# Variance of a head from a sum of squares and a column of the gates product, and column sums of two weights in other tiles

## The chip, the cores and the metric

The kernel runs on one core of one Trainium2 chip. The metric is the device time of one execution in microseconds (us). The engines are TensorE (PE; PEld is its loading of weights), VectorE (DVE), ScalarE (ACT), GpSimd (POOL) and SyncE (SP), which issues the DMA transfers.

## What is computed

One decoder layer in fp32 on x of 16 x 256 x 512, in three parts, each followed by a layer norm without parameters:

```python
x = _layernorm(x + attn(x))            # a state space block: projections, convolution, scan, output product
x = _layernorm(x + xattn(x, k, bias, ctx))   # long convolutions of v*x2 by k, contracted with x1
x = _layernorm(x + ffn(x))             # base product, plus low-rank updates of the best 2 of 8 experts
```

The layer norm and the last part, which the change touches, are

```python
m = mean(x); v = var(x); (x - m) / sqrt(v + 1e-5)
base   = x_flat @ W.T + b
logits = x_flat @ gate_w.T + gate_b
gates  = softmax(top_k(logits, 2))
out    = base + sum over the two experts of gate * (x_flat @ lora_A.T) @ lora_B.T
```

## The kernel before

**Two stages.** The first (the first 766 us or so) is the state space block over 8 groups of 512 tokens, with its layer norm; its result goes to DRAM. The second is a loop over 32 heads (`h`); a head is 8 channels of the sequence for all 16 batches, so it has 128 rows of 512. It does the long convolution of the head as matmuls, the contraction, the second layer norm, and the feed-forward part with the third norm. The order of instructions on each engine is that of the source (the schedule is manual). Buffers rotate within pools: a tile that takes a buffer waits for the readers of the one before.

**A round of the head loop** works on three heads. For head h it convolves two halves of the batches, q = 0 and q = 1, into four PSUM banks `y0`, `y1` (two each). Each half begins with a seed product (`seeded`, L1006, into `y1`), whose result ACT copies into another block (`spread_seed`, L1010). Then PE does four full products (L1021) and twelve quadrant products (L1036); the last quadrants wait for a tiny ACT copy `one` (L1052). DVE contracts a half with two products with the context (`multiplied`, L1071, `y1` first) and two reductions (`reduced`, L1081). As there is one set of `y` banks, the seed of one half waits until the products of the half before have read `y1`. For head h+1 DVE forms `kv` (`products`, L155), and POOL forms `xs` (twice, L991), the difference of filters `Td` (L996) and the skip products `sk` (L927).

For head h-1 the round finishes the second half: POOL adds `ol` (L1229), which holds its output with channels on partitions: four chunks of 128 channels by 128 rows. The mean over channels needs no subtraction from `ol`: the weights `w_f` (of the base product) and `w_gl` (8 gate columns and 128 low-rank columns) have had their column means removed once, in group 1 of the first stage. What is left of the second layer norm is one scale per row, `rs`, from the variance. For this, `centre` (L1175) transposes the four chunks of `ol` on PE (`transposed`, L1108, identity as the weights' partner), so that a row lies along a partition; ACT sums the transposed rows (L1181), POOL makes the negative mean `nm_b` (L1094), ACT squares the centred rows and sums (L1099), and POOL forms `var_b` (L1101) and its power of -1/2, `rs_b` (L1102). The POOL work of the next residual (`skip_term` L944, `with_residual` L958 and L962) stands between `nm_b` and `var_b`, or behind `rs_b`.

Then PE does the gates product `gl` (L1272: four chunks, 136 columns) and the base product (L1196, in parts around the seed). `gates` on DVE scales the logits (`lg`, L1115), takes their maximum (L1117), ranks them by three comparisons of 64 elements (`cmp`, L1124 to L1126) and a reduction (L1128), zeroes the exponentials of all but two (`ex`, L1130), and scales the low-rank product (`xa`, L1135). In the next round `xa` is transposed (L1186), copied by ACT (L1188) and multiplied into `base` (L1192); `finish` forms `x3` with its sum on DVE (L1148), then the centred square of the third norm, by the same `centred_squares` (L1094 to L1102 with tag c), and `store` writes the result (L1158, L1159). The last head has its own code after the loop, with transposes and a statistics instruction of DVE.

**The column means** are formed by `chunk_sum` (POOL, L525 and L527) and `centred` (PE L533 into the PSUM tile `mw`, DVE L535), called in group 1 at i = 3 to 6. The sums lie in two of the six rotating buffers of tag `acc`; the convolutions of the first stage (ACT L578, DVE L580 and L582) use the same six. `mw` is one of two buffers of the pool `ps_t`, which `head_means` (PE L593, `xm`) and others use.

Of the kernel before, what the change touches and what calls it, by code (L numbers as in the profile page):

```python
# [10 lines left out]
ALU = mybir.AluOpType  # L11
# [39 lines left out]
    (3, 1, 1), (2, 1, 1), (1, 1, 1), (0, 1, 1),  # L51
)
ER = NE * R
WARM = 8


# [14 lines left out]
def decoder_kernel(  # L71
# [108 lines left out]
    with ExitStack() as s1:  # L180
# [7 lines left out]

        xg = x.rearrange("b (c p) d -> (b c) p d", p=P)
        xTg = xT.rearrange("(k p) n -> p k n", p=P)  # L190
        NG = NTOK // GT

        def load_x(g):
            xs = []
# [326 lines left out]

        def chunk_sum(w, cols):

            total = p2.tile([P, D], F32, tag="acc", name="w_sum", bufs=6)[:, 0:cols]
            nc.gpsimd.tensor_tensor(total, w[:, 0, :], w[:, 1, :], ALU.add)  # L525
            for kc in range(2, KD):
                nc.gpsimd.tensor_tensor(total, total, w[:, kc, :], ALU.add)  # L527
            return total

        def centred(w, cols, total):  # L530

            ps = ps_t.tile([P, 512], F32, tag="tr", name="mw")
            nc.tensor.matmul(ps[:, 0:cols], share, total, start=True, stop=True)  # L533
            for kc in range(KD):
                nc.vector.tensor_tensor(w[:, kc, :], w[:, kc, :], ps[:, 0:cols], ALU.subtract)  # L535

        def normalised(g, *ts):

# [5 lines left out]

        heads = {}
        late, sums = [], []
        for g in range(NG):
            xs = xs_next
            more = g + 1 < NG
            if not more:  # L550
                load_w_o(0, 1)
                cTs = [load_c(0), load_c(1)]
# [92 lines left out]
            for i, (kind, p) in enumerate(order):  # L645
                if g == 1 and i == 2:
                    with_identity(w_f)
                if g == 1 and i in (3, 4):
                    w, cols = ((w_f, D), (w_gl, NE + ER))[i - 3]
                    total = chunk_sum(w, cols)  # L650
                if g == 1 and i in (5, 6):
                    centred(*sums.pop(0))
                if g == 1 and i in (3, 4):
                    sums.append((w, cols, total))
                if i == 6:
                    ms = [head_means(0)]
                if g == 0 and i == 0:
                    al, be = first_products(
                        kinds[kind], p, True, None,
                        lambda: begun.append(begin_products(w_xi, order[1][1], False)),  # L660
                    )
                else:
                    al, be = first_products(
                        kinds[kind], p, i % 3 == 0, begun.pop(0) if begun else None
                    )
                if i == 8:
                    ms.append(head_means(1))
                if i == 9:


                    yps = ps_t.tile([P, S], F32, tag="tr", name="yps")
                    for ht in range(HT):
                        for b in range(GB):
                            nc.tensor.matmul(
                                yps[b * HP : (b + 1) * HP],
                                sel[:, ht].rearrange("p q h -> p (q h)"),
                                Bs[ht][:, b * S : (b + 1) * S],
                                start=(ht == 0),
                                stop=(ht == HT - 1),
                            )  # L680
                if before is not None:
                    finish_products()
                to = places(kind, p)
                u = first_sums(al, be, to)
                if i == 8:
                    states(1, stepped(ms[1], spreads[2]), spreads[3])
                if i == 6:
                    ms = [stepped(ms[0], spreads[0])]
                    spreads.append(spread(1, 1))
                if g == 0:  # L690
                    if i == 1:
                        parts = decays()
                    if i == 2:
                        nc.scalar.activation(A, A, AF.Exp)
                        nc.vector.tensor_scalar(A, A, -1.0, None, ALU.mult)
                    if i in (1, 2, 4):
                        next(parts)
                if i == 9:
                    yT = q3.tile([P, S], F32, tag="vn", name="yT", bufs=1)
                    nc.scalar.copy(yT, yps)  # L700
                if before is not None:
                    finish_sums((lambda: next(parts)) if g == 0 and i == 2 else None)
                if g == 0 and i == 3:
                    next(parts)
                if g == 0 and i in later:
                    for n, (w, k) in enumerate(later[i]):
                        ins = weight_sums(nc.gpsimd, w, k)
                        if n == 0:
                            wait_for(ins, mixes[-1])
                if i == 7:  # L710
                    states(0, ms[0], spreads[1])
                if i == 8:
                    outputs(0)
                    outputs(1)
                    if more:
                        rt = to_dram(rms(xs_next))
                    if g == 0:
                        behind = []
                        w_sums = w_o_sums(behind)
                        next(w_sums)  # L720
                before = (kind, p, al, be, u, to)
                if i < 2 and late:
                    normalised(g - 1, late.pop(0))
                if i == 1 and more:
                    xs_next = load_x(g + 1)
# [163 lines left out]
            if g == 0:  # L889
                skip_bc = wp.tile([P, S], F32, name="skip_bc")  # L890
                nc.sync.dma_start(skip_bc, skip.partition_broadcast(P))
                w_gl = wp.tile([P, KD, NE + ER], F32, name="w_gl")
                nc.sync.dma_start(w_gl, WglT.rearrange("(k p) e -> p k e", p=P))
                w_f = wp.tile([P, KD, D], F32, name="w_f")
                nc.sync.dma_start(w_f, WffnT.rearrange("(k p) o -> p k o", p=P))
                b_bc = wp.tile([P, D], F32, name="b_bc")
# [14 lines left out]
    with ExitStack() as s2:  # L911
# [190 lines left out]
            nc.gpsimd.tensor_tensor(rs, var, nhalf[:, 0:1], ALU.pow)  # L1102
            return nm, rs

        def transposed(src):
            tr = ps_t.tile([P, KD, P], F32, tag="tr", name="tr")
            for kc in range(KD):
                nc.tensor.transpose(tr[:, kc, :], src[kc], ident)  # L1108
            return tr

        def gates(gl, rs):


# [20 lines left out]
            xa = p2.tile([P, NE, R], F32, tag="xa", name="xa")  # L1134
            nc.vector.scalar_tensor_tensor(  # L1135
                xa,
                gl[:, NE:].rearrange("p (e r) -> p e r", r=R),
                den,
                ex.unsqueeze(2).to_broadcast([P, NE, R]),
                ALU.mult,  # L1140
# [1 line left out]
            )  # L1142
            return xa

        def finish(h, base, rs):
            x3 = p2.tile([P, D], F32, tag="x3", name="x3")
            total = p2.tile([P, 1], F32, tag="sum_c", name="sum_c")
            nc.vector.scalar_tensor_tensor(  # L1148
                x3, base, rs, b_bc, ALU.mult, ALU.add, accum_out=total
            )  # L1150
            nm, rs = centred_squares(x3, total, "c")
            nb = p2.tile([P, 1], F32, tag="nb", name="nb")
            nc.gpsimd.tensor_tensor(nb, nm, rs, ALU.mult)
            return h, x3, nb, rs
# [17 lines left out]
            vns.append(load_v(2))  # L1172
            cTs.append(load_c(2))

        def centre(o_l, between):  # L1175

            tr = transposed([o_l[:, lc, :] for lc in range(NL)])
            src = tr.rearrange("p c l -> p (c l)")
            sq = p2.tile([P, D], F32, tag="sq", name="sq")
            total = p2.tile([P, 1], F32, tag="sum_b", name="sum_b")  # L1180
            nc.scalar.activation(sq, src, AF.Identity, accum_out=total)  # L1181
            return centred_squares(src, total, "b", between)[1]

        def turned_gates(xa, at=None):
            xat = (at or ps_t).tile([ER, P], F32, tag="vp" if at else "tr", name="xat")
# [15 lines left out]
        for h in range(HX):  # L1201
# [23 lines left out]
            if ff:  # L1225
# [6 lines left out]
                    red_f.rearrange("p q k t -> p k q t"),  # L1232
                    ALU.add,
                )
            ready = finish(*done) if done is not None else None
            red = p2.tile([P, NQ, NL, BQ * NH], F32, tag="red", name="red")
            convolve(y, kv, T, Td, 0, late=h == 0, ahead=ahead)
            if h == 0:
# [22 lines left out]
            def meanwhile():  # L1261
                skips.append(skip_term(cT, ws, behind))

            if ff:
                rs = centre(o_l, meanwhile)
            else:
                meanwhile()
            o = with_residual(skips[0], vT)
            if ff:
                gl = ps_t.tile([P, NE + ER], F32, tag="tr", name="gl")  # L1270
                for kc in range(KD):
                    nc.tensor.matmul(  # L1272
                        gl, o_l[:, kc, :], w_gl[:, kc, :], start=(kc == 0), stop=(kc == KD - 1)
                    )
                base = ps_b.tile([P, D], F32, tag="base", name="base")
                feed_forward(base, o_l, (0,), True)
            if nxt:
# [30 lines left out]

        o_f, red_f, y_f, cT_f = last
        tr = ps_t.tile([P, KD, P], F32, tag="tr", name="tr")  # L1310
        gl = ps_b.tile([P, NE + ER], F32, tag="vp", name="gl")
        o_l = {}

        def contracted(src, ks):
# [31 lines left out]
        def norms_and_gates(*ks):  # L1346
            for k in ks:
                nc.tensor.transpose(tr[:, k, :], own(k), ident)
            for k in ks:
                nc.tensor.matmul(  # L1350
                    gl, own(k), w_gl[:, k, :], start=(k == 0), stop=(k == 3),
                    skip_group_check=True,
                )

# [101 lines left out]
```

## Time and profile before

| | |
|---|---|
| time, median of 3 runs | 1436.82 us (1436.52 to 1436.96) |
| time of the profiled execution | 1436.9 us |
| its span | 1435.1 us |
| granted PE clock, mean | 0.996 of full |
| busy: PE, DVE, POOL, ACT | 1415.7, 1209.7, 470.6, 438.1 us |
| transposes of `ol` (L1108), 124 | 20.3 us busy |
| gates product (L1272), 248 passes | 33.9 us busy |
| ACT passes over the transposes (L1181, L1099), 31 each | 18.5 and 21.4 us |

The page gives for each engine its busy time, and for groups of instructions the mean duration of one; the timeline gives them in order of time, with the idle time before one and what ended it. An fp32 matmul leaves two records (two passes), a transpose one. Ends of matmuls are modelled, and a busy PE is not PE at its peak. A busy DVE includes time in which an instruction has begun but stands still.

### The profile page before, as it was taken

To read this page: it belongs to the slowest core of one execution; us is meant where nothing else is said; L and a number is where in the kernel's file an instruction comes from. 1 tells how busy PE (TensorE), PEld (TensorE's weight loads), DVE (VectorE), ACT (ScalarE), POOL (GpSimd) and SP (SyncE) were. 2 spreads that over 40 slices of the span, in tenths; PEclk is the share of its full clock that TensorE was granted. 3 is DMA by queue.
4 is the path that set the end of the run, shared out by engine and by line. 5 is a ranking of instruction groups with operands and counts; after the bars stand their busy time and mean duration, and the time that the engine had idled before them with its cause. 6 is when DMAs were issued, how large, how long until landed. Compare 5 with 4: busy or idle time off the path is not lost.

```text
span 1435.1 us, 19011 instructions
## 1 busy us (share of the span) xinstructions
PE 1415.7 (99%) x6944; PEld 914.7 (64%) x6944; DVE 1209.7 (84%) x2102; ACT 438.1 (31%) x962; POOL 470.6 (33%) x661
## 2 busy tenths in 40 slices
PE   9999999999999999999999999999999999999997
PEld 7887788888888888888884444444444444444443
DVE  6988788878788787877847999999999999999996
ACT  2423223233232232332311333233323333333331
POOL 5452010010100201001003564556455545554552
PEclk9999999999999999999999999999999999999999
DMA  8114021120121111212003112221221122112200
GB/s 299 33 39 130 8 63 65 37 83 8 39 81 45 54 36 38 83 34 94 16 16 107 63 47 74 67 64 55 70 71 61 58 66 74 54 65 66 74 27 23
DMA packets 49166, 89.18 MB, mean 62 GB/s; under 512 B 8880, under 2 KB 13360, under 8 KB 49072
## 3 DMA queue, kind: packets, MB, share of 16 engines
q1 hardware_dynamic: 49072, 87.96, 19.2%
q8 instruction: 55, 0.90, 0.3%
q14 instruction: 39, 0.32, 0.1%
HBM read 70.62 MB, written 17.32 MB: 61 GB/s over the span
## 4 chain that ended last, share of the span: by engine, by line
PE 96%; DVE 2%; issue 1%; POOL 1%; DMA 0%; ACT 0%; POOLq 0%; SPq 0%; DVEq 0%
PE mm L328 20%; PE y L1021 15%; PE s L328 14%; PE y L1036 12%; PE base L1196 7%; PE s L778 6%; PE mm L778 6%; PE y L1006 4%; PE gl L1272 2%; PE base L1192 2%; PE tr L1108 1%; PE tr L145 1%; PE xm L593 1%; PE mm L735 1%; PE mm L869 1%; PE s L869 1%
## 5 line engine op out<-in xcount | busy, mean ns | idle before, releaser
L1071 DVE TENSOR_TENSOR pr<-y,cT 128x1024 f32<-128x1024 f32 x126 | 148.2, 1217 | 47.1 <-PE y L1036 47.1
L1036 PE MATMUL y<-kv 64*64 64x512 f32 x1536 | 179.6, 598 | 0.0
L582 DVE SCALAR_TENSOR_TENSOR acc<-xi,wc,acc 128x512 f32<-128x512 f32 x192 | 142.0, 753 | 9.8 <-ACT acc L578 4.1
L1081 DVE TENSOR_REDUCE red<-pr 128x128 f32<-128x1024 f32 x126 | 147.1, 1208 | 0.0
L155 DVE TENSOR_TENSOR kv<-tr,cT 128x1024 f32<-128x1024 f32 x124 | 145.4, 1213 | 0.0
L1021 PE MATMUL y<-kv 128*128 128x512 f32 x272 | 128.2, 594 | 0.6 <-ACT y L1010 0.4
L1036 PEld LDWEIGHTS y<-kv 64*64 64x64 f32 x1536 | 52.2, 132 | 119.0 <-issue 96.9
L1196 PE MATMUL base<-w_f,ol 128*128 128x512 f32 x248 | 121.4, 593 | 0.0
L1021 PE MATMUL y<-kv,Td 128*128 128x512 f32 x248 | 116.5, 592 | 0.0
L66 POOL TENSOR_TENSOR rs_a<-ve_a,nhalf 128x1 f32<-128x1 f32 x32 | 19.0, 594 | 243.0 <-DVE ve_a L64 243.0
L389 POOL TENSOR_TENSOR rstd<-ms,nhalf 128x4 f32<-128x4 f32 (+1 forms) x9 | 8.5, 948 | 258.9 <-DVE ms L387 258.9
L1021 PEld LDWEIGHTS y<-kv 128*128 128x128 f32 x272 | 51.1, 190 | 66.4 <-issue 48.9
L1229 POOL TENSOR_TENSOR ol<-o,red 128x512 f32<-128x512 f32 x31 | 39.4, 1272 | 161.7 <-DVE red L1081 161.7
L328 PE MATMUL mm<-XT,w_z 128*128 128x256 f32 x384 | 90.7, 379 | 0.0
L1021 PEld LDWEIGHTS y<-kv,Td 128*128 128x128 f32 x248 | 47.1, 190 | 59.3 <-issue 59.3
L991 POOL TENSOR_TENSOR xs<-kv 128x512 f32<-128x512 f32 x63 | 80.2, 1274 | 2.4
L1010 ACT COPY y<-y 64x512 f32<-64x512 f32 x124 | 69.2, 558 | 34.7 <-PE y L1006 28.9
L328 PEld LDWEIGHTS mm<-XT,w_z 128*128 128x128 f32 x384 | 73.0, 190 | 9.9
L328 PE MATMUL mm<-xnT,w_z 128*128 128x256 f32 x288 | 71.0, 382 | 0.0
L1006 PE MATMUL y<-xs,kv 128*128 128x512 f32 x124 | 64.8, 604 | 2.6 <-DVE pr L1071 1.6
L1196 PEld LDWEIGHTS base<-w_f,ol 128*128 128x128 f32 x248 | 42.5, 190 | 30.9 <-issue 30.9
L328 PE MATMUL s<-XT,w_xi 128*128 128x256 f32 x256 | 61.0, 380 | 0.6 <-DVE XT L224 0.5
(278 smaller groups left out, 2827.3 us busy)
## 6 DMA issues: line engine op xcount, KB each, us to landing
cT<-in_ctxT SPq DMA_DIRECT2D x32, 384.0 KB
kv<-in_toep SPq DMA_DIRECT2D x32, 384.0 KB
xt<-in_x SPq DMA_DIRECT2D x32, 256.0 KB
spread<-both SPq DMA_DIRECT2D x32, 256.0 KB
first<-xt SPq DMA_DIRECT2D x32, 256.0 KB
vn<-first SPq DMA_DIRECT2D x32, 256.0 KB
out<-res SPq DMA_DIRECT2D x31, 256.0 KB
xnT<-in_xT SPq DMA_DIRECT2D x7, 1024.0 KB
```

Of the source, the lines that this page charges most:

```text
L155: last = nc.vector.tensor_tensor(kv[:, q, k * BQ : (k + NL // 2) * BQ], vT[:, q, blks].rearrange("p k (b i) -> p (k b) i", i=NH).unsqueeze ...
L328: nc.tensor.matmul(ps, w[:, p, a, kc, :], Xs[b][:, kc, :], start=start and kc == 0, stop=stop and kc == 1, skip_group_check=upon,)
L582: ins = nc.vector.scalar_tensor_tensor(acc, xi[:, :, k : k + S], wc[:, c, k : k + 1], acc, ALU.mult, ALU.add)
L778: nc.tensor.matmul(ps, own[a][c][:, n * P : (n + 1) * P], w_o[b][c], start=start and c == 0, stop=stop and c == HC - 1, skip_group_check=upon,
L991: return nc.gpsimd.tensor_tensor(xs[:, q], moving(kv, q, 0), moving(kv, q, 1), ALU.add)
L1006: nc.tensor.matmul(bank_of(y, 3), T[:, SHARED_AT, :], xs[:, q], start=True, stop=True)
L1010: nc.scalar.copy(bank_of(y, 2)[b : b + HP], bank_of(y, 3)[a : a + HP])
L1021: nc.tensor.matmul(bank_of(y, lb), w, moving(kv, q, mb), start=not late and lb not in begun, stop=False, skip_group_check=True,)
L1036: return nc.tensor.matmul(bank_of(y, lb)[cols], T[rows, DIAGONAL_AT, (b - a) * HP : (b - a + 1) * HP], moving(kv, q, lb)[rows], start=star ...
L1071: nc.vector.tensor_tensor(pr.rearrange("p (k b j) i -> p k b j i", k=2, j=NH), y[i].rearrange("p k (b j i) -> p k b j i", j=NH, i=NH), cT[ ...
L1081: nc.vector.tensor_reduce(red[:, q, 2 * i : 2 * i + 2, :].rearrange("p k t -> p (k t)"), pr, AX.X, ALU.add)
L1196: nc.tensor.matmul(base, o_l[:, kc, :], w_f[:, kc, :], start=(first and kc == kcs[0]), stop=False)
```

## The change

It has two parts.

In the head loop the transposes go, and with them `centre`. The variance of a row is formed as the mean of squares less the square of the mean. `w_gl` gets a 137th column that holds 1/512 in every entry, so that the gates product gives the mean of each row beside the logits. For the squares, ACT squares `ol` as it lies, POOL folds the four chunks into one by two additions in place, and a matmul with one column of `share` (entries 1/512) sums over the partitions into a 138th column of `gl`. ACT squares the mean (`m2`; it is made to wait for that last product), DVE forms mean of squares + 1e-5 - `m2` in one instruction, and POOL raises it to -1/2. The square of `ol` is issued right behind `ol`, ahead of `finish`; the folds stand inside `finish`, between `nm_c` and the square of x3; the products, `m2`, the variance and the power stand behind `with_residual`, where the gates product stood.

In the first stage, the column sum of `w_f` takes the buffer of tag `vn` (one buffer, otherwise `yT` and `vn`), and that of `w_gl` a tile of its own, in place of two of the six `acc` buffers.

```diff
+NG = NE + ER
 def chunk_sum(w, cols):
-    total = p2.tile([P, D], F32, tag="acc", name="w_sum", bufs=6)[:, 0:cols]
-    nc.gpsimd.tensor_tensor(total, w[:, 0, :], w[:, 1, :], ALU.add)
+    if cols == D:
+        total = q3.tile([P, D], F32, tag="vn", name="w_sum", bufs=1)
+    else:
+        total = p1.tile([P, cols], F32, name="g_sum")
+    nc.gpsimd.tensor_tensor(total, w[:, 0, 0:cols], w[:, 1, 0:cols], ALU.add)
...
-    w_gl = wp.tile([P, KD, NE + ER], F32, name="w_gl")
-    nc.sync.dma_start(w_gl, WglT.rearrange("(k p) e -> p k e", p=P))
+    w_gl = wp.tile([P, KD, NG + 1], F32, name="w_gl")
+    nc.gpsimd.memset(w_gl[:, :, NG:], 1.0 / D)
+    nc.sync.dma_start(w_gl[:, :, 0:NG], WglT.rearrange("(k p) e -> p k e", p=P))
...
-def transposed(src):
-    tr = ps_t.tile([P, KD, P], F32, tag="tr", name="tr")
-    for kc in range(KD):
-        nc.tensor.transpose(tr[:, kc, :], src[kc], ident)
-    return tr
...
-def finish(h, base, rs):
+def finish(h, base, rs, between=None):
...
-    nm, rs = centred_squares(x3, total, "c")
+    nm, rs = centred_squares(x3, total, "c", between)
...
-def centre(o_l, between):
-    tr = transposed([o_l[:, lc, :] for lc in range(NL)])
-    src = tr.rearrange("p c l -> p (c l)")
+def squares(o_l):
     sq = p2.tile([P, D], F32, tag="sq", name="sq")
-    total = p2.tile([P, 1], F32, tag="sum_b", name="sum_b")
-    nc.scalar.activation(sq, src, AF.Identity, accum_out=total)
-    return centred_squares(src, total, "b", between)[1]
+    nc.scalar.activation(sq, o_l.rearrange("p k t -> p (k t)"), AF.Square)
+    def folded():
+        for n in (D // 2, D // 4):
+            nc.gpsimd.tensor_tensor(sq[:, 0:n], sq[:, 0:n], sq[:, n : 2 * n], ALU.add)
+    return sq[:, 0:P], folded
+
+def products_with_gates(o_l, sq):
+    gl = ps_t.tile([P, NG + 2], F32, tag="tr", name="gl")
+    for kc in range(KD):
+        nc.tensor.matmul(
+            gl[:, 0 : NG + 1], o_l[:, kc, :], w_gl[:, kc, :],
+            start=(kc == 0), stop=(kc == KD - 1),
+        )
+    last = nc.tensor.matmul(
+        gl[:, NG + 1 :], sq, share[:, 0:1], start=True, stop=True, skip_group_check=True
+    )
+    m2 = p2.tile([P, 1], F32, tag="m2", name="m2")
+    wait_for(nc.scalar.activation(m2, gl[:, NG : NG + 1], AF.Square), last)
+    return gl, m2
+
+def spread_of(gl, m2):
+    var = p2.tile([P, 1], F32, tag="var_b", name="var_b")
+    nc.vector.scalar_tensor_tensor(
+        var, gl[:, NG + 1 :], LN_EPS, m2, ALU.add, ALU.subtract
+    )
+    rs = p2.tile([P, 1], F32, tag="rs_b", name="rs_b")
+    nc.gpsimd.tensor_tensor(rs, var, nhalf[:, 0:1], ALU.pow)
+    return rs
...
+        sq, folded = squares(o_l)        # right behind ol
-    ready = finish(*done) if done is not None else None
+    if done is not None:
+        ready = finish(*done, folded)
+    else:
+        ready = None
+        if ff:
+            folded()
...
-    if ff:
-        rs = centre(o_l, meanwhile)
-    else:
-        meanwhile()
+    meanwhile()
     o = with_residual(skips[0], vT)
     if ff:
-        gl = ps_t.tile([P, NE + ER], F32, tag="tr", name="gl")
-        for kc in range(KD):
-            nc.tensor.matmul(
-                gl, o_l[:, kc, :], w_gl[:, kc, :], start=(kc == 0), stop=(kc == KD - 1)
-            )
+        gl, m2 = products_with_gates(o_l, sq)
+        rs = spread_of(gl, m2)
```

The last head keeps its own code; it reads columns 0 to 135 of `w_gl`. On each engine the order of the other instructions stays as it is.

## The prediction

> **What bounds the kernel now.** I read the page's first part, then a table by stage, one head in order of time, and last the list of waits for the one long stall. TensorE is busy nearly everywhere:
>
> ```profile
> PE 1415.7 (99%) x6944; PEld 914.7 (64%) x6944; DVE 1209.7 (84%) x2102; ACT 438.1 (31%) x962; POOL 470.6 (33%) x661
> 1000.00:1100.00 100.00, 100.00 (x469) 43.30 (x468) 92.00 (x123) 31.54 (x76) 53.60 (x77) 1.00 0.20 64
> ```
>
> The second line is a stretch of the head loop (columns: window, its length, busy PE, PEld, DVE, ACT, POOL, granted clock, DMA share, GB/s). PE is at 100%, but DVE is at 92%, so I look at one head in order of time (start, duration, engine, line, operation, idle before):
>
> ```profile
> 1097.89 0.42 PEld L1108 LDWEIGHTS tr<-ident,ol 128*128 128x128 f32 x4 [0.81 <-issue]
> 1098.00 2.36 DVE L1071 TENSOR_TENSOR pr<-y,cT 128x1024 f32<-128x1024 f32 x2 [1.35 <-PE y L1036]
> 1098.28 1.00 PEld L1272 LDWEIGHTS gl<-w_gl,ol 128*128 128x128 f32 x8
> ...
> 1103.91 1.27 POOL L991 TENSOR_TENSOR xs<-kv 128x512 f32<-128x512 f32 x1
> 1104.78 0.22 DVE L1115 SCALAR_TENSOR_TENSOR lg<-gl,rs_b,gb_bc 128x8 f32<-128x8 f32 x1
> 1105.11 0.22 DVE L1124 TENSOR_TENSOR cmp<-lg 128x64 f32<-128x64 f32 x1
> 1105.14 0.77 POOL L996 TENSOR_TENSOR Td<-kv 128x256 f32<-128x256 f32 x1
> 1105.24 0.75 DVE L1125 TENSOR_TENSOR cmp<-lg 128x64 f32<-128x64 f32 x1
> 1105.87 1.49 POOL L927 TENSOR_TENSOR sk<-kv,skip_bc 128x512 f32<-128x512 f32 x1
> 1105.91 1.53 DVE L1126 TENSOR_TENSOR cmp<-cmp,tri 128x64 f32<-128x64 f32 x1
> 1107.31 1.28 POOL L991 TENSOR_TENSOR xs<-kv 128x512 f32<-128x512 f32 x1
> 1107.88 0.74 DVE L1130 SCALAR_TENSOR_TENSOR ex<-rank,ex 128x8 f32<-128x8 f32 x1
> 1109.13 2.34 DVE L1071 TENSOR_TENSOR pr<-y,cT 128x1024 f32<-128x1024 f32 x2
> 1110.48 1.06 PE L1006 MATMUL y<-xs,kv 128*128 128x512 f32 x2
> ```
>
> Call T the start of the transposes (1097.89); the next head's are at 1118.50, and every head from 1 to 30 takes 20.60 or 20.61 us. Two chains run from T to the seed matmul at T+12.6. On PE the work is back to back. On DVE the products at T+0.1 (which waited 1.35 us for PE) are followed without a gap by reductions, kv products, gates, and the products of the other half at T+11.23. The seed overwrites y1, which the first of those reads: by the single records it ends at T+12.45, and the seed's weights load at T+12.52. **So this stretch is bound by PE and DVE at once**, within about 0.05 us. From the seed to the next T (8.0 us) PE alone decides; DVE has its 1.35 us there.
>
> Inside the gates, tiny DVE operations last as long as the POOL operation beside them: L1125 ends 0.08 after Td, L1126 0.08 after sk, L1130 with the second xs. In the last head, with POOL silent, the single records give 0.21, 0.22, 0.22 and 0.17 us for L1124, L1125, L1126, L1130.
>
> The second place is in group 1 of the first stage:
>
> ```profile
> 141.07 0.72 ACT L578 ACTIVATE acc<-xi,wc 128x512 f32<-128x512 f32 x1 [5.65 <-PE mw L533]
> 141.82 2.33 DVE L582 SCALAR_TENSOR_TENSOR acc<-xi,wc,acc 128x512 f32<-128x512 f32 x3 [2.34 <-ACT acc L578]
> 144.07 2.47 DVE L535 TENSOR_TENSOR w_f<-w_f,mw 128x512 f32<-128x512 f32 x4
> 146.59 1.93 PE L593 MATMUL xm<-acc,mean 128*32 128x512 f32 x8 [5.56 <-DVE w_f L535]
> 143.00:148.00 5.00, 1.41 (x8) 0.20 (x8) 4.89 (x10) 0.63 (x1) 0.00 (x0) 0.63 0.00 0
> ```
>
> ACT waits for a buffer of `acc` until PE has read the column sum lying in it; DVE waits for ACT; PE waits for DVE to empty the bank it wants. Afterwards the granted clock is one half for 6.83 us, from 144.28 to 151.11.
>
> **What the skill says.** "SBUF — State Buffer", section "Who interferes with whom": a DVE instruction with two SBUF inputs contends with a GpSimd instruction that reads SBUF, and the later one fully blocks. The trace agrees: the four gate operations above have both inputs in SBUF; L1071 and L155 (one in PSUM) never stretch. In the records whoever starts first wins: L1126, 40 ns behind sk, loses; in head 31 L1125, 54 ns ahead of L962, takes 0.21. "TensorE: Matmul & The Clock Gate", Part 1: the clock halves after an idle window of about 3.4 us, the windows run freely. The trace agrees: 6.83 is two of them.
>
> **The change, part by part.**
>
> PE, per head: four transposes go: 1097.89 to 1098.28 by their weight loads, −0.39. The gates product has 137 columns for 136 in eight passes; a pass takes 0.115, so +0.007. The one-column product has no row before. Bounds: nothing (loads all hidden), or two loads of 0.19 (L1272); as its passes cover nothing, I take two exposed loads at the skill's columns/1.2 (same page, "LDWEIGHTS"): an estimate of 0.21. Net −0.17, in the stretch where DVE is equally long, so worth nothing unless DVE shortens too.
>
> ACT: the Identity pass (0.60+0.19) and the centred square (0.69+0.19) go; a square of `ol` (about 0.62 like L385) comes right after `ol`, in 2.65 us in which ACT waits for `nm_c`. It pushes x3's square by about 0.35; that ends 0.37 before L1052 `one` is due, so nothing; without this cover the quadrants, which wait for `one`, would slip. `m2` (about 0.2) waits for the one-column product; behind it are the store and the spread copies, which need the later seed product anyway: nothing.
>
> POOL: nm_b and var_b (0.22+0.19) go; two folds of 256 and 128 come: 0.77 (Td's row) and, by the step to 1.27 at 512, 0.52. They end about 1.3 us before T, where PE needs them 0.9 after T: hidden. But the order changes: t and the three o's no longer queue behind nm_b (which waited to T+1.47); they run from about T−0.1 and end near T+3.3. rs_b now waits for DVE's new variance.
>
> DVE: one `var_b` instruction, about 0.21 like L1115, between the reductions and the kv products; neighbours overlap by 0.08, so it delays kv and gates by 0.13 (bounds: nothing, if it vanished in the overlap, or the whole 0.21). Behind it on DVE stand the kv products and the gates, and PE's seed waits for these; its own wait, for `m2`, is over 2.8 us before.
>
> Now the gates. The second reduction ends at T+4.71; var_b ends T+4.83; the power starts 0.09 later (as L66 behind L64) and takes 0.57; neighbours on POOL overlap by 0.03, so its first xs starts at T+5.46, where it was T+6.02. The four POOL operations take 4.68 to their end as before: T+10.14 for T+10.70. But DVE arrives 0.13 later. L1124 used to run in the gap between xs and Td, L1125 before sk, L1126 before the second xs, L1130 behind it. Now L1124 comes (T+7.35) about when Td ends, so L1125 waits for sk (0.04 to 0.05 us behind its start) and L1126 for the second xs. From that end: 0.08, rank and the way to L1130 0.43, L1130 to `xa` 0.41, to the products 0.27: T+11.33 for T+11.23. **Earlier POOL, later DVE: +0.10 us a head**, 30 heads, +3.0. The seed follows DVE, PE waits there about 0.3. In head 31 nothing of this binds and PE's 0.2 counts: −0.2.
>
> Column sums: POOL's work is the same, in buffers nobody waits for. ACT's L578 starts when its input is there (136.72), not at 141.07; DVE's six L582 run through; L535 ends at 144.10 instead of 146.54. PE resumes 2.4 earlier, at 144.15; it still waits 3.3, because the bank of `mw` is emptied only then. The half clock now costs 2.25 (from 146.59 to 151.11, halved). If the window falls at 144.28 again, one busy window lifts it: 1.7, so −0.55; if 3.3 us of idleness fill no window, −2.25. I take −1.2. Together −3.6. The load of `w_gl` into rows of 137 and a memset of four columns lie 12 us before use: nothing.
>
> Sum: −3.6 + 3.0 − 0.2 = −0.8. The profiled execution took 1436.9 (span 1435.1, 1.8 around it), so 1436.1; the runs' median is 0.1 lower: **1436.0 us**.
>
> **Rivals.** (a) *PE decides after all*: L1125 gets in ahead of sk (margin 0.05), L1126 and L1130 then wait one POOL operation each as now, and the products come 0.53 behind POOL's end, T+10.67. Then PE bounds: 31×0.17=5.3 gained, with −3.6: about 1428. For it: the margin. Against: L1126 lost with the same margin in every head. (b) *Slower*: L1124 also misses its gap and starts behind sk; then L1126 runs only after the second xs and L1125: +0.14 more, 0.24 a head, 7.2−0.2−3.6=+3.4: 1440.2. It decides from 0.03 us: var_b longer, or POOL earlier, by that. (c) *The buffers don't do what the change says*: ACT finds another `acc` buffer held. Then +2.8: 1439.6. Against: group 2, with the same turns and no sums, has no such wait.
>
> **How the numbers follow.** Main case 0.45, own range 1433.5 to 1438.5 (clock between −0.55 and −2.25, head between +0.05 and +0.16); (a) 0.24; (b) 0.20; (c) 0.04; the rest spread. A difference under 0.2% (2.9 us) can't be told from none. Faster: (a), a tenth of the main case, some rest: 0.32. Slower: (b), a little of the main case and the rest: 0.28. Same: 0.40. The range over all, 1428 to 1441, reaches to both (a) and (b).
>
> **What would show it.** Right: a head of 20.65 to 20.75; seeds waiting for pr; L1126 ending with the second xs, L1130 at 0.17; PE's wait at L593 near 3.3. Wrong: a head of 20.43 (a), 20.84 (b), or L578 still waiting 5 us (c). A PE wait on the folded squares or on `one` would be a cover gone that I count as safe.

## The result, and the profile after

The kernel after takes 1433.56 us (median of 16 runs, 1432.09 to 1434.59), beside 1436.30 us of the kernel before on the same chip (16 runs): ratio 0.998, 95% interval 0.9972 to 0.9987. So it is faster, by about 2.7 us: the interval lies below one, though the size, 0.19%, is just under the 0.2% (2.9 us) that I had taken as the least that can be told from none. It is inside my range of 1428 to 1441 and at the very end of the main case's own (1433.5 to 1438.5). The forecast was 1436.0, a gain of 0.8. The sign was right; of the two opposed terms in the sum, the loss in the heads was nearly four times too large. (One experiment below, `before_hold`, was profiled in an execution at about half clock throughout, 2480.11 us with a mean granted clock of 0.556; its timeline is therefore read from a second profile of the same kernel, `before_hold_look`.)

The engines' busy times of the kernel after, from its page:

```profile
PE 1414.5 (99%) x6882; PEld 908.0 (63%) x6882; DVE 1210.5 (85%) x2133; ACT 414.5 (29%) x900; POOL 492.3 (34%) x662
1000.00:1100.00 100.00, 100.00 (x459) 42.72 (x452) 92.03 (x126) 29.63 (x69) 56.75 (x78) 1.00 0.21 66
```

62 PE instructions and 62 of ACT are gone and 31 of DVE have come, but the second line, the same 100 us of the heads as before (columns: window, its length, busy PE, PEld, DVE, ACT, POOL, granted clock, DMA share, GB/s), still has PE at 100 and DVE at 92.

The spans differ by 3.02 us (1435.11 and 1432.09). By the records it divides so:

| part | predicted | measured in the two profiles |
|---|---|---|
| up to the first `xm` product of stage 1 | nothing | -0.60 |
| from there to the first `xm` product of group 1: PE's wait | -2.4 | -2.54 |
| from there to that of group 2: half clock | -1.2 | -0.51 |
| 30 heads | +3.0 | +0.8 (20.604 to 20.629 us each) |
| after the last seed | -0.2 | -0.13 |

The stretch from group 2 to the first seed is the same in both, 530.95 us. The -0.60 at the start belongs to the pair of executions: over the twelve profiles of this study that product starts between 46.5 and 47.6, without regard to the change, and before's was the latest but one.

Stage 1, group 1, in order of time (start, duration, engine, line, operation, idle before and what ended it), kernel after:

```profile
136.05 0.72 ACT L583 ACTIVATE acc<-xi,wc 128x512 f32<-128x512 f32 x1 [1.34 <-DVE xi L373]
136.45 4.56 DVE L587 SCALAR_TENSOR_TENSOR acc<-xi,wc,acc 128x512 f32<-128x512 f32 x6
140.93 2.47 DVE L540 TENSOR_TENSOR w_f<-w_f,mw 128x512 f32<-128x512 f32 x4
143.46 1.83 PE L598 MATMUL xm<-acc,mean 128*32 128x512 f32 x8 [3.03 <-DVE w_f L540]
```

ACT's pass waits for its input alone (1.34 for 5.65), DVE's six run through, the four subtractions follow at once, and PE's wait is 3.03 for 5.56. It still ends with `w_f`.

One head, kernel after; T, where the gates product now begins, is 1094.60:

```profile
1099.22 0.15 DVE L1204 SCALAR_TENSOR_TENSOR var_b<-gl,m 128x1 f32<-128x1 f32 x1
1099.29 2.34 DVE L156 TENSOR_TENSOR kv<-tr,cT 128x1024 f32<-128x1024 f32 x2
1099.52 0.56 POOL L1208 TENSOR_TENSOR rs_b<-var_b,nhalf 128x1 f32<-128x1 f32 x1 [1.65 <-DVE var_b L1204]
1100.04 1.27 POOL L997 TENSOR_TENSOR xs<-kv 128x512 f32<-128x512 f32 x1
...
1101.88 0.22 DVE L1124 TENSOR_TENSOR cmp<-lg 128x64 f32<-128x64 f32 x1
1101.95 1.49 POOL L933 TENSOR_TENSOR sk<-kv,skip_bc 128x512 f32<-128x512 f32 x1
1102.01 1.51 DVE L1125 TENSOR_TENSOR cmp<-lg 128x64 f32<-128x64 f32 x1
1103.39 1.27 POOL L997 TENSOR_TENSOR xs<-kv 128x512 f32<-128x512 f32 x1
1103.44 1.31 DVE L1126 TENSOR_TENSOR cmp<-cmp,tri 128x64 f32<-128x64 f32 x1
1105.18 0.17 DVE L1130 SCALAR_TENSOR_TENSOR ex<-rank,ex 128x8 f32<-128x8 f32 x1
1105.90 2.34 DVE L1077 TENSOR_TENSOR pr<-y,cT 128x1024 f32<-128x1024 f32 x2
1107.18 0.30 PEld L1012 LDWEIGHTS y<-xs,kv 128*128 128x128 f32 x2 [0.56 <-issue]
```

This is the main case, line by line: xs at T+5.44 (predicted 5.46), L1125 as long as sk, L1126 as long as the second xs, L1130 at 0.17, the products at T+11.30, and the seed's load behind the first of them. The loading of weights stands idle for 0.56 us ahead of that load. Not all of this is a wait for DVE, as the same place in the kernel before shows:

```profile
1110.41 0.30 PEld L1006 LDWEIGHTS y<-xs,kv 128*128 128x128 f32 x2 [0.33 <-issue]
```

There it is 0.33, and 0.33 again below in `after_hold`, where DVE is early. In the kernel after the median over heads 1 to 30 is 0.51 (the head shown is the longest, 20.67 us), so the products make PE wait 0.18 us more a head, where I had given it 0.3.

### The profile page after: what moved, and what is told of

Read it like the earlier page. It is cut to its first block, busy times and chain, and to the rows that moved or that the text cites. A ratio compares the mean times of both kernels' runs of the same rounds, so it can differ in the third digit from the quotient of the medians.

```text
span 1432.1 us, 18826 instructions
## 1 busy us (share of the span) xinstructions
PE 1414.5 (99%) x6882; PEld 908.0 (63%) x6882; DVE 1210.5 (85%) x2133; ACT 414.5 (29%) x900; POOL 492.3 (34%) x662
## 4 chain that ended last, share of the span: by engine, by line
PE 87%; DVE 2%; issue 1%; POOL 1%; ACT 0%; POOLq 0%; DVEq 0%
PE mm L329 16%; PE y L1027 15%; PE y L1042 12%; PE s L329 11%; PE base L1223 8%; PE s L783 5%; PE mm L783 5%; PE y L1012 4%; PE gl L1190 2%; PE base L1219 2%; PE tr L146 1%; PE xm L598 1%; PE mm L740 1%; PE mm L874 1%; PE s L874 1%
```

## The experiments

Line numbers shift by a few from kernel to kernel; the names of operands stay. The length of a head is the mean of the intervals between seeds of the same half, over heads 1 to 30. "First `xm` to group 2" is the time from group 1's first `xm` product to group 2's, which is free of what the start brings.

**One part of the change at a time.** `sums_only` is the kernel before with the new `chunk_sum` alone, `var_only` the kernel after with the old one:

```diff
-    if cols == D:
-        total = q3.tile([P, D], F32, tag="vn", name="w_sum", bufs=1)
-    else:
-        total = p1.tile([P, cols], F32, name="g_sum")
+    total = p2.tile([P, D], F32, tag="acc", name="w_sum", bufs=6)[:, 0:cols]
```

(this is `var_only`; `sums_only` is the reverse, on the kernel before).

> The kernel before with only the column sums moved to other tiles. Theory: the whole gain is here. Group 1 of stage 1 loses 2.5 us of PE's wait ahead of the first xm product (5.56 to about 3.0) and 0.5 us or more of half clock, the heads stay as before (period 20.60). Median 3.0 to 3.6 us under the kernel before, so 0.5 to 0.9 us under the kernel after. Rival: the gain of 2.8 us is partly a luckier start and a gain in the heads; then the sums alone give 2 us or less.

> The kernel after with the column sums back in the acc tiles, so only the variance is changed. Theory: a head goes from 20.60 to 20.63, thirty of them make +0.8, the last head gives back 0.1; PE's wait ahead of the first xm product is 5.5 again. Median 0.4 to 1.0 us over the kernel before, within what can be told from no change. Rival (the saved PE work counts): 0.17 a head, 5 us under the kernel before.

Measured, beside the kernel before at 1436.45: `sums_only` 1433.04 (ratio 0.9978, 0.9969 to 0.9986), `var_only` 1436.83 (1.0003, 0.9995 to 1.0011). PE's first `xm` product in the timeline of `sums_only`, then of `var_only`:

```profile
143.07 1.94 PE L596 MATMUL xm<-acc,mean 128*32 128x512 f32 x8 [3.12 <-DVE w_f L538]
```

```profile
146.18 1.93 PE L595 MATMUL xm<-acc,mean 128*32 128x512 f32 x8 [5.57 <-DVE w_f L537]
```

Heads: 20.605 and 20.630. So the whole gain, 3.4 us, is that of the two buffers; the new variance, which is most of the diff, brings nothing that can be told from no change, and its +0.4 has the sign of +0.026 x 30 - 0.13 = +0.65. The two parts add up to the whole (-3.4 + 0.4 = -3.0, measured -2.7), so neither hides the other. Both rivals fall.

**Is it VectorE, waiting for GpSimd, that takes the saved PE work?** In `after_hold` sk, and the second xs behind it in GpSimd's queue, wait until the last small gates instruction `ex` is done:

```diff
-                sk_next = skip_sums(h + 1, kv_n)
-                more_next[2](1)
             if ff:
                 xa = gates(gl, rs)       # picked: the instructions `ex`
+            if nxt:
+                sk_next = skip_sums(h + 1, kv_n, picked[-1] if ff else None)
+                more_next[2](1)
...
+            if behind is not None:
+                wait_for(ins, behind)      # ins: the product sk
```

`before_hold` is the same edit in the kernel before.

> The kernel after, with GpSimd's product sk and the second xs behind it held until the last small gates instruction (ex) of the head, so that VectorE does the five small gates instructions without GpSimd in between. Theory: the head is set by VectorE's chain up to the gate products, which now waits 1.3 us twice for GpSimd; freed of it, the products start at about T+9 in place of T+11.3, the seed no longer waits for them and PE sets the head: 20.40 to 20.45, about 6 us under the kernel after. Rival 1 (PE sets the head already): no change. Rival 2 (the two GpSimd products only move and delay the gate products or the next head's skip sums by as much): a head of 20.6 or more.

> The kernel before with the same hold. Theory: PE had at most 0.05 us of slack in a head of the kernel before, so the head goes from 20.60 to 20.55 at best, 0 to 2 us under the kernel before; the difference between this and the held kernel after, beside the 3 us of the column sums, is what the four transposes are worth on PE once VectorE doesn't set the head: 0.1 to 0.17 a head, 3 to 5 us. Rival (the transposes lie in idle time of PE anyway): both held kernels have the same head.

> The kernel before with sk held, as in before_hold, for a profile at full clock. Theory: PE sets the head here without VectorE, at 20.55 to 20.60; the idle time ahead of the seed is gone or has only moved, and VectorE has over 1 us of idle time a head that it doesn't have in the kernel before. Rival (the hold does nothing in this kernel): the gates instructions still wait for GpSimd.

Measured: `after_hold` 1426.51 (ratio 0.9937, 0.9924 to 0.9951), `before_hold` 1436.26 (1.0000, 0.9991 to 1.0008). `before_hold_look` gave 1435.41 in one run, beside 1436.95. Heads: 20.447 in `after_hold`, 20.603 in `before_hold_look`. A head of `after_hold`, in order of time (its T is about 1090.0):

```profile
1097.27 0.21 DVE L1126 TENSOR_TENSOR cmp<-lg 128x64 f32<-128x64 f32 x1
1097.40 0.22 DVE L1127 TENSOR_TENSOR cmp<-lg 128x64 f32<-128x64 f32 x1
1097.53 0.22 DVE L1128 TENSOR_TENSOR cmp<-cmp,tri 128x64 f32<-128x64 f32 x1
1098.44 1.49 POOL L933 TENSOR_TENSOR sk<-kv,skip_bc 128x512 f32<-128x512 f32 x1 [1.06 <-DVE ex L1132]
1101.05 2.36 DVE L1079 TENSOR_TENSOR pr<-y,cT 128x1024 f32<-128x1024 f32 x2 [2.06 <-PE y L1044]
1102.34 0.30 PEld L1014 LDWEIGHTS y<-xs,kv 128*128 128x128 f32 x2 [0.33 <-issue]
```

The three `cmp` instructions take 0.21 to 0.22 us each in place of 0.22, 1.51 and 1.31, and DVE then waits 2.06 us for PE, where in the kernel after it had no idle time. DVE's busy time falls from 1210.5 to 1142.6, 2.3 us a head with the same instructions: that much of its "busy" was standing still. The same place in `before_hold_look`:

```profile
1103.77 0.75 DVE L1127 TENSOR_TENSOR cmp<-lg 128x64 f32<-128x64 f32 x1
1104.44 0.21 DVE L1128 TENSOR_TENSOR cmp<-cmp,tri 128x64 f32<-128x64 f32 x1
1105.34 1.50 POOL L927 TENSOR_TENSOR sk<-kv,skip_bc 128x512 f32<-128x512 f32 x1 [0.90 <-DVE ex L1132]
1107.64 2.36 DVE L1073 TENSOR_TENSOR pr<-y,cT 128x1024 f32<-128x1024 f32 x2 [1.80 <-PE y L1038]
```

There too DVE now waits for PE, 1.80 us (L1127 still stands beside Td, which is not held), and the head doesn't move: in the kernel before PE decides by itself at 20.60. So both held kernels are bound by PE, and their heads differ by 0.156, which is what the new variance saves on PE: the -0.17 of the prediction. In the kernel after it is lost to DVE. One expectation missed: the products did not begin at T+9 but at T+11.07 (in all thirty heads), since they need PE's quadrants of the second half, which are done only then; the gain in the head is as expected all the same. The 7.05 us between the medians of `after_hold` and the kernel after is more than its heads explain (30 x 0.182 = 5.5); for the rest the clock is the likely cause, to which I come below.

**How much slack PE has.** The transposes are put back on PE, four and two of them, with nobody reading them:

```diff
+    tr = ps_t.tile([P, KD, P], F32, tag="tr", name="tr")
+    for kc in range(KD):          # range(2) in after_transposes_2
+        nc.tensor.transpose(tr[:, kc, :], o_l[:, kc, :], ident)
     gl = ps_t.tile([P, NG + 2], F32, tag="tr", name="gl")
```

> The kernel after with the four transposes put back on PE ahead of the gates products, their output read by nobody (added work only). Theory: PE has 0.18 us of slack in a head of the kernel after (20.63 against 20.45 with GpSimd held), so 0.39 us of transposes cost 0.39 - 0.18 = 0.21: head 20.82 to 20.86, 6 us over the kernel after. Rival (PE has no slack): 21.02. Rival (transposes lie in idle time anyway): 20.63.

> The same with two of the four transposes. Theory: 0.20 us more on PE just fill the slack of 0.18: head 20.63 to 20.66. Rival (no slack): 20.83.

Measured (one profiled execution each): heads of 20.838 and 20.627. Two transposes cost nothing (20.629 without), four cost 0.209. From PE's own bound, 20.447, four cost 0.391, so 0.098 each; two at this price would reach 20.643, so the first two cost a little less, at most 0.09 each. Of the three cases in the expectations, only the slack of 0.18 fits both runs.

**Does L1124 lose its place, as the slower rival had it?** Two more one-element instructions stand in front of DVE's kv (their results are not used):

```diff
+    for n in range(2):
+        more = p2.tile([P, 1], F32, tag="var_more", name="var_more")
+        nc.vector.scalar_tensor_tensor(
+            more, gl[:, NG + 1 :], LN_EPS, m2, ALU.add, ALU.subtract
+        )
```

> The kernel after with two more instructions of one element like the one for the variance, ahead of VectorE's kv (added work only). Theory, as the second rival of the prediction has it: each delays VectorE by about 0.06 us; the first small gates instruction, which began 0.07 us ahead of GpSimd's sk, then misses its place and waits for sk; head 20.63 + 0.12 + about 0.14, so 20.80 to 20.95. If no place is missed: 20.72 to 20.78. If VectorE isn't what sets the head: 20.63.

A head of `after_var3` in order of time:

```profile
1103.45 1.49 POOL L933 TENSOR_TENSOR sk<-kv,skip_bc 128x512 f32<-128x512 f32 x1
1103.52 1.50 DVE L1124 TENSOR_TENSOR cmp<-lg 128x64 f32<-128x64 f32 x1
1104.88 1.29 POOL L997 TENSOR_TENSOR xs<-kv 128x512 f32<-128x512 f32 x1
1104.94 1.30 DVE L1125 TENSOR_TENSOR cmp<-lg 128x64 f32<-128x64 f32 x1
1106.17 0.21 DVE L1126 TENSOR_TENSOR cmp<-cmp,tri 128x64 f32<-128x64 f32 x1
```

L1124 now starts 0.06 to 0.08 us behind sk in every one of the thirty heads (in the kernel after 0.05 to 0.08 ahead of it) and waits for it; L1125 waits for xs; L1126 comes when both are over. The head is 20.759: +0.13. My expectation was 20.80 to 20.95, too high, and instructive: I added the delay of the two instructions (kv begins 0.13 later) to the price of the lost place. But the second xs ends at the same time after T, 10.07 in the kernel after and 10.06 here, and the gates end behind it; so the delay itself costs nothing, and what is paid is one `cmp` instruction of 0.21 behind the xs in place of beside it. The head alone could not have told this: 20.759 also lies in the 20.72 to 20.78 that I gave for no place missed. The records decide, since they show the place lost in every head and the end of xs where it was.

**Stage 1: the wait that is left.** In `after_mw_copy` ACT copies the means of `w_f` out of their PSUM bank, and DVE's four subtractions move behind the first sums of the next piece:

```diff
     nc.tensor.matmul(ps[:, 0:cols], share, total, start=True, stop=True)
+    if cols == D:
+        nc.scalar.copy(total, ps)
+        return
+    less(w, cols, ps)             # the subtractions
...
     u = first_sums(al, be, to)
+    if g == 1 and i == 5:
+        less(*whole)              # those of w_f, from total
```

`after_awake` leaves the order and puts twelve unread 128x128 products on PE behind the small `mw` product, inside PE's wait:

```diff
     nc.tensor.matmul(ps[:, 0:cols], share, total, start=True, stop=True)
+    if cols < D:
+        for _ in range(12):
+            nc.tensor.matmul(
+                ps[:, 256:384], ident, ident, start=True, stop=True,
+                skip_group_check=True,
+            )
```

> The kernel after, with the column means of w_f copied by ACT from their PSUM bank to SBUF, and VectorE's four subtractions (2.47 us) moved behind the first sums of the next piece, so that PE's first xm product needn't wait for them. Theory: PE's wait of 3.0 us ahead of the first xm product falls below 0.5, and no window of half clock follows it (3.4 us long in the kernel after, 1.6 us dearer than none): 3 to 4.7 us under the kernel after. Rival (the wait passes to the next thing that VectorE is late with, xi): 0 to 1.5 us under.

> The kernel after with twelve unread products of 128x128 on PE ahead of the first xm product of group 1 (added work only, inside PE's wait of 3.0 us). Theory: the half clock in stage 1 comes from a window in which PE has too little to do, as chance places the windows; with the added work it never comes, and PE's path isn't longer: from group 1's first xm product to group 2's takes 91.9 to 92.1 us in place of 93.6, median 0.5 to 2 us under the kernel after. Rival (the half clock has another cause, or the added work delays the product): same or slower.

Measured, beside the kernel before at 1436.56: `after_mw_copy` 1428.91 (ratio 0.9948, 0.9935 to 0.9960), `after_awake` 1432.26 (0.9970, 0.9958 to 0.9981). Timeline of `after_mw_copy`, then of `after_awake`:

```profile
136.92 0.57 ACT L539 COPY w_sum<-mw 128x512 f32<-128x512 f32 x1
140.61 1.06 PE L605 MATMUL xm<-acc,mean 128*32 128x512 f32 x8
142.48 2.49 DVE L547 TENSOR_TENSOR w_f<-w_f,w_sum 128x512 f32<-128x512 f32 x4
```

```profile
140.81 2.84 PE L540 MATMUL mw<-ident 128*128 128x128 f32 x24
144.00 1.06 PE L604 MATMUL xm<-acc,mean 128*32 128x512 f32 x8 [0.35 <-DVE w_f L546]
```

With the copy, PE's product has no wait at all, and the eight records of it take 1.06 us for 1.83: no half clock. The time between the first `xm` products of groups 0 and 1 falls from 96.45 to 93.36 (-3.09), first `xm` to group 2 from 93.61 to 91.96 (-1.65): 4.74 together, 4.65 between the medians. `after_awake` gets the second part alone (91.96), with the wait only filled, and its median is 1.3 us lower. The rivals fall: in `after_mw_copy` no wait passed on to the next instruction, and in `after_awake` the added work didn't delay the product (96.37 after that of group 0, for 96.45).

The half clock in stage 1 is thus a matter of how idle PE is, but of where the windows lie too. In the twelve profiles a stretch of half clock in group 1 lasts 3.41 or 6.83 us. I counted windows of 3.413 us from the moment at which the clock is first released, which differs from execution to execution (5.5 to 11.2 us). Three profiles with the same wait of 3.0 us, in this order: `after`, `after_transposes_2`, `after_hold` (columns as above; the last but two is the granted clock):

```profile
140.20:143.62 3.42, 0.39 (x6) 0.18 (x9) 3.38 (x7) 0.63 (x1) 0.00 (x0) 1.00 0.00 0
143.62:147.03 3.41, 3.41 (x12) 1.52 (x5) 2.44 (x9) 0.96 (x2) 0.00 (x0) 0.50 0.00 0
```

```profile
138.95:142.36 3.41, 1.25 (x7) 0.94 (x5) 3.34 (x6) 0.88 (x2) 0.00 (x0) 1.00 0.00 0
142.36:145.77 3.41, 2.56 (x10) 0.81 (x11) 3.27 (x11) 0.93 (x2) 0.00 (x0) 0.50 0.00 0
145.77:149.19 3.42, 3.42 (x10) 2.71 (x9) 0.19 (x1) 0.03 (x1) 0.00 (x0) 0.50 0.00 0
```

```profile
138.58:142.00 3.42, 1.60 (x9) 1.24 (x7) 3.35 (x6) 1.23 (x3) 0.00 (x0) 1.00 0.00 0
142.00:145.41 3.41, 2.21 (x14) 1.25 (x15) 3.27 (x9) 0.59 (x2) 0.00 (x0) 1.00 0.00 0
```

In `after` the idle stretch falls into one window (PE busy 0.11 of it), and the next runs at half clock. In `after_transposes_2` a window busy to 0.37 was enough, and the half clock stayed for a second window, since the first was busy only to 0.75. In `after_hold` the same idleness is split over two windows (0.47 and 0.65), and the clock stays full. In the wait of 5.56 us, every one of the three profiles that have it (`before`, `var_only`, `before_hold_look`) holds a nearly empty window (0.05, 0.00, 0.00), and each is followed by half clock. Its price differs too: first `xm` to group 2 is 94.12, 93.44 and 93.43, so 2.2 us over the 91.96 without half clock in the profile of the kernel before, and 1.5 in the two others.

**Both edits together.** `both_mended` is the kernel after with the held sk and the copied means.

> The kernel after with GpSimd's sk held until ex and the copied means of w_f. Theory: the gains add, since one lies in stage 1 and one in the heads: 5.5 from the heads and 3 to 4.7 from stage 1, so 1423 to 1425.5. Rival (the copied means bring nothing): 1426.5, as with the held sk alone.

Measured: 1423.45 us (1423.43 to 1423.84), ratio 0.9909, 0.9894 to 0.9924. It beats both kernels, the kernel before by 13.1 us. By the records its head is 20.447 and first `xm` to group 2 91.96. Over the kernel after it gains 10.1 us by the medians, which is the sum of 5.5 from the heads and 4.65 in stage 1. Its four runs lie within 0.4 us, those of the kernel after within 2.5. A half clock that comes or not would make such a spread, but it is not the only source: the five runs of `after_mw_copy`, whose PE has no wait there either, lie within 1.0, and the six of `after_awake` within 1.1. It would explain the 7.05 of `after_hold` too, whose five runs lie in two groups, three at 1426.0 to 1426.5 and two at 1428.3 to 1428.9; its profiled execution, at 1426.51, was one without half clock. The mean granted clock on record agrees: in the profiles it is 0.996 or 0.997 with a half clock in group 1, and 0.998 or 0.999 without; the three faster runs of `after_hold` have 0.999, the two slower ones 0.997 and 0.998. Of the kernel after, the eleven runs at 0.996 or 0.997 have a median of 1433.84, the five at 0.998 one of 1432.32. This supports the half clock as the cause, but the runs without a profile do not show where it fell.

## Why the prediction was right or wrong

**What bounds a head: right.** "Bound by PE and DVE at once": taking DVE's standing away moved the kernel before by nothing and the kernel after by 0.182 a head. In the kernel before the products began at T+11.23 with DVE standing and at T+11.22 without, when PE was done with the quadrants, so the two were 0.01 apart. "So worth nothing unless DVE shortens too" is what `var_only` and `after_hold` show.

**PE's saving, -0.17: right.** 0.156 between the two held kernels. The four transposes are 0.391 by `after_transposes`, predicted 0.39; the one-column product, for which I estimated 0.21 from the Trainium skill, "TensorE: Matmul & The Clock Gate", section "LDWEIGHTS (loading the stationary operand)", comes out as 0.391 - 0.156 - 0.007 = 0.23. Its two loads are 0.30 us busy in the timeline.

**The gates: right in mechanism, wrong in size; the failing term is "the four POOL operations take 4.68 to their end as before".** They take 4.63 (mean of thirty heads, 4.68 before). The 0.05 lies between Td and sk: Td takes 0.73 for 0.78. In the kernel before L1124 begins 0.03 ahead of Td, which is then held up; now it comes 0.6 behind the start of Td. (The kernels of the experiments agree: 0.78 in `sums_only` and `before_hold_look`, where this instruction begins ahead of Td, and 0.73 in `var_only`, `after_hold` and `after_var3`, where it begins behind it.) I had counted what POOL does to DVE and not what DVE did to POOL. The first xs begins 0.57 earlier, predicted 0.56. With the two, the second xs ends 0.63 earlier in place of 0.56, and the products begin 0.03 later than before in place of 0.10 (means of thirty heads, from T). The step from the end of xs to the products is 1.19 as worked out. The head follows with +0.025, and thirty heads cost 0.8 and not 3.0. So the head of 20.629 lies outside the 20.65 to 20.75 that I had named as the sign of being right, and its step outside the main case's +0.05 to +0.16. Between the two profiles these 2.2 us are as large as the whole error of the forecast; the other differences (-0.1 of the wait, +0.7 of the clock, -0.6 of the start, +0.1 of the last head) cancel, and that is luck.

**var_b's delay of 0.13: wrong, without consequence.** It took 0.15, not 0.21, and kv begins 0.07 later. `after_var3` shows why that doesn't matter to the time: GpSimd's end decides. It does matter to the margin of L1124.

**The rivals.** (a) needed L1125 ahead of sk: it wasn't, in any head from 1 to 30. (b) was near: the margin was 0.05 to 0.08 us, and where it is overdrawn, the price is +0.13, predicted +0.14. (c) is excluded by ACT's 1.34.

**Column sums.** The wait: -2.54 for -2.4, with 3.03 left for "near 3.3". The clock: -0.51 in the profiled pair for -1.2, near the -0.55 that I had named for "one busy window lifts it". Together, -3.4 by the medians of `sums_only` for -3.6. As a forecast for a median the single number was the wrong kind: by the windows above, the old wait of 5.56 leaves one window idle for at least 2.78 us of its 3.41, however the windows lie (half of the wait, when it is split evenly over two), and so at most 0.19 busy; the new one of 3.03 gives an idle enough window only in part of their positions.

**The start** was left at nothing, rightly for the medians; it makes the profiled pair look 0.6 better.

## What to carry to other kernels

Two engines that end a stretch together must both be relieved before either saving shows; hold one back by an experiment and read the other's own period, as the held kernels did here. When tiny VectorE instructions stand as long as the GpSimd instruction beside them, hold the GpSimd work back by a wait and leave the VectorE work where it is: one such wait brought 5.5 us in the kernel after, where PE had 0.18 us of slack a head, and nothing in the kernel before, where it had none. And when an order between two engines is turned, count what each did to the other, since the one that no longer waits gives time back.

## What the runs showed of the hardware

- VectorE and GpSimd hold each other up in both directions. The Trainium skill, "SBUF — State Buffer", section "Who interferes with whom", says that the order of issue decides who is blocked. The traces agree: L1124 took 0.22 us where it began 0.05 to 0.08 ahead of sk (the kernel after) and 1.50 where it began 0.06 to 0.08 behind it (`after_var3`), and where it began ahead of Td, GpSimd's Td took 0.78 for 0.73.
- A VectorE instruction of one element (`var_b`) took 0.15 us and delayed the next by 0.06 to 0.07.
- The Trainium skill, "TensorE: Matmul & The Clock Gate", Part 1, has the clock halve after an idle window and return after a busy one. In these profiles the window needn't be idle: PE busy for 0.37 and 0.42 of a window (`after_transposes_2`, `after_var3`) was followed by half clock, 0.45 to 0.47 (`var_only`, `before_hold_look`, `after_transposes`, `after_hold`) was not. A half-clock window busy to 0.75 (`after_transposes_2`) or 0.32 (`before`) did not bring the full clock back, one of 0.92 did (`var_only`, `before_hold_look`). Busy times here are from modelled ends of matmuls, and twelve profiles are few.
- This chance, worth 0 to 2.9 us in the profiles with the new wait (91.96 to 94.84 from group 1 to group 2), has the size of the spread between runs: 2.5 us among the 16 of the kernel after, 0.4 and 1.0 among the 4 and 5 of the two kernels whose PE has no such wait (`both_mended`, `after_mw_copy`).
